# A 0.5 moved into a bias, one row added earlier, fewer sums by DMA, and ScalarE's operand left in the bank where TensorE wrote it

## The chip, the cores and the metric

The kernel runs on one core of a Trainium2 chip. A core has a matrix engine (TensorE, PE in the profile), VectorE (DVE), ScalarE (ACT) and GpSimd (POOL), each with its own queue of instructions that it works off in order, and 16 DMA engines. The metric is the device time of one execution in microseconds, and less is better. A time within 0.5% of the kernel before counts as the same here.

## The reference

The input x holds 64 graphs of 256 nodes with 128 features each, all in float32, and there is one 256 x 256 matrix adj. Four layers follow each other; each takes h = relu(layernorm(x)) and adds its result to x.

```python
# layer 0: five steps of a gated update, h = (1 - z) h + z hv, with adj @ h as message
# layer 1: x + relu([h, A h, A(A h) ...] @ Theta1 + bias)
# layer 2: y = ((adj @ h) + h) @ weight + bias;  x + y / max(norm(y), 1e-12)
# layer 3:
s1 = einsum('bkf,ef->bke', h, W1)          # W = adj, cut in two halves
s2 = einsum('bkf,ef->bke', h, W2)
pre = s1[:, :, None, :] + s2[:, None, :, :] + b_lin
e = einsum('bije,e->bij', leaky_relu(pre, 0.2), a) + adj
x + sigmoid(softmax(e) @ h)
```

Layer 3 is nearly all of the work: for each of 64 graphs it forms 256 x 256 pairs of nodes with 256 channels each, bends them, and sums them over the channels with weights a. The kernel writes sigmoid(v) as 0.5 tanh(v/2) + 0.5, and this last 0.5 is the "0.5 of x" in the title.

## The kernel before, in words

The graphs go through in 32 pairs. For each pair, `front` (L484) computes layers 0 to 2 and prepares layer 3; it is a chain of some 109 steps, each on one engine, with a `yield` between them that names the engine and the time from which the step can run. Front p is begun when pair p - 2 begins to be scored, and the planner spreads its steps over the scores of 1.8 pairs (`SPREAD`), so that two fronts are under way beside the main work. At its end a front leaves the operands of layer 3: s1a, s1b (rows, used as one scalar for each partition), s2c and s2n (copies in SBUF, for GpSimd) and s2a, which stays in the PSUM bank where TensorE projected it, since VectorE reads it from there.

The main work is cut into slots: 64 slots for each pair, 2048 in all, and each has two tiles of 128 x 2048 elements, one for each half of the channels (k = 0 and k = 1). `work_on_tile` (L910) makes a tile: VectorE in one instruction (L930, k = 0 only, from s1a and the bank of s2a), ScalarE in eight instructions (L942, k = 1 only), GpSimd in eight instructions (L947, either half). ScalarE reads its operand in a PSUM bank of its own, `S2P`, that is kept for the whole program: TensorE projects s2n into a common bank, ScalarE copies it to SBUF (L765), and before its first tile of a pair ScalarE copies it again, from SBUF into the bank S2P (L937; L774 for the first pair, whose graphs run alone). There are 14 tile buffers.

`score` (L991) has TensorE sum a tile over its channels, in four groups of 32 columns, into one row of a bank of scores (L1006). One slot in three is "joined" (`SHARE = (1, 3)`, none in the last 96 slots): GpSimd makes its second tile, and issues a DMA that adds this tile onto the first one in SBUF (`add_pair`, L965, the issue is L967); TensorE then scores one tile instead of two. 650 slots are joined.

When the 64 tiles of 32 slots are scored, `tail` (L805) finishes them: two VectorE instructions add the smaller of two rows to the scores in the bank (L812), one adds the row `lin` and writes the sum to SBUF (L816); then come the maximum, the exponential, two transposes by TensorE, a product with h3, tanh on ScalarE (L849), and o = 0.5 tanh + x3 (L853). So x3 must hold the 0.5 already: GpSimd adds it for each pair (L713), behind the layernorm that reads x3.

The order of the whole program is written out by a planner, the loop at the end. It keeps a clock for each engine, gives each step a cost from a table (`ran(engine, us)`), and takes for the engine whose clock is least what is ready: tails first, then fronts, then tiles or scores. Each engine is bound to the resulting order. Costs that matter here: TURN (four transposes) 0.80 us, PROJECT (one tile scored, or one projection) 0.86, norm on GpSimd 1.55, L713 0.7, one issue 0.65, landing of a sum 6.6 after its issue. Eight PSUM banks lie in a list `spare`; `take()` (L121) gives the one that is free the longest, and a step that needs a bank isn't ready while the list is empty.

Of the kernel before, what the change touches and what calls it, by code (L numbers as in the profile page):

```python
# [10 lines left out]
OP = mybir.AluOpType  # L11
# [10 lines left out]
MOST_POSITIVE = -MOST_NEGATIVE  # L22
PE, DVE, ACT, POOL = ENGINES = (mybir.EngineType.PE, mybir.EngineType.DVE, mybir.EngineType.Activation, mybir.EngineType.Pool)
SLOTS = 64
SHARE = (1, 3)
AHEAD_OF = 2
ALONE = 96
LOW = 1
# [4 lines left out]
def kernel(  # L33
# [87 lines left out]
    def take():  # L121

        spare.sort(key=lambda b: b[1])
        return spare.pop(0)
# [139 lines left out]
    def other_constants():  # L264
# [17 lines left out]
        yield DVE, 12.0  # L282
        nc.vector.tensor_add(th[:, 1:3, :], th_raw[:, 1:3, :], th_raw[:, 3:5, :])
        nc.vector.tensor_sub(th[:, 0, :], th_raw[:, 0, :], th[:, 2, :])
        ran(DVE, 0.5)
        yield DVE, clock[DVE]
        small = work.tile([P, 32], F32, name="small", bufs=1)

# [164 lines left out]
    SHORT = dict(tag="short", bufs=12)  # L453


    PROJECT, MIX, TURN, PRODUCT, PRODUCTS = (None, 0.44, 0.86), (None, 0.88, 1.74), (None, 0.55, 0.80), (None, 0.45, 0.88), (None, 1.33, 2.64)
    COPY, BIASED, TANH, ELEMENTS = (None, 0.32, 0.48), (None, 0.40, 0.58), (None, 0.40, 0.57), (None, 0.36, 0.61)
    NORMED, STATS, LAST = (None, 0.78, 1.55), (None, 0.40, 0.8), (None, 0.55, 1.04)

    def norm(src, since, h):  # L460

        nb = src.shape[1]
        stats = work.tile([P, nb * NC, 3], F32, name="stats", bufs=4)
        mv = work.tile([P, nb * NC, 2], F32, name="mv", bufs=4)
        s, h = rows_of(src), rows_of(h)[:, :, 0:D]
        yield DVE, since
        for k in range(0, nb * NC, 2):
            nc.vector.bn_stats(stats[:, k:k + 2, :].rearrange("p k s -> p (k s)"), s[:, k:k + 2, :].rearrange("p k d -> p d k"))
        nc.vector.tensor_reduce(mv[:, :, 0], stats[:, :, 1:2], AX.X, OP.add, negate=True)
        t = ran(DVE, STATS[nb], since) + 0.1  # L470
        yield POOL, t
        inverse_root(mv[:, :, 1], stats[:, :, 2], 1.0 / D, OP.mult, LN_EPS, OP.add)
        nc.gpsimd.tensor_mul(mv[:, :, 0], mv[:, :, 0], mv[:, :, 1])  # L473
        t = ran(POOL, 1.55, t)
        yield ACT, t
        for k in range(nb * NC):
            nc.scalar.activation(h[:, k, :], s[:, k, :], AF.Relu, bias=mv[:, k, 0:1], scale=mv[:, k, 1:2])  # L477
        return ran(ACT, NORMED[nb], t)

    READY = {}  # L480
    S2P = []
    OF_FIRST = {}

    def front(p, batches):  # L484
# [34 lines left out]
        def turned_of(b):  # L519
            return by_token(b[0], nb)  # L520
# [143 lines left out]
        t = ran(DVE, ELEMENTS[nb], t)  # L664
        yield DVE, t
        x2 = token("x2", tag="x12", bufs=3)
        nc.vector.scalar_tensor_tensor(x2, turned_of(po), 0.0, x1, op0=OP.max, op1=OP.add)
        t = ran(DVE, ELEMENTS[nb])
        spare.append([po[0], t])

# [38 lines left out]
        h3 = kept("h3", [NC, D + 1])  # L709
        nc.gpsimd.memset(h3[:, :, :, D:D + 1], 2.0)  # L710
        t = yield from norm(x3, t, h3)
        yield POOL, t
        nc.gpsimd.tensor_scalar(x3, x3, 0.5, None, op0=OP.add)  # L713
        ran(POOL, 0.45 if alone else 0.7, t)
        yield PE, t, 1
        b = take()
        to_feature(b[0], h3)
# [39 lines left out]
        t = moved(t) + 1.5  # L757
        t_lin = t
        yield PE, t_hT, 1
        b = take()  # L760
        project(b[0], w2n[:, P:2 * P], hT)
        t = ran(PE, PROJECT[nb], t_hT, b[1])
        yield ACT, t
        s2n = kept("s2n", [N])
        nc.scalar.copy(s2n, seen(b))  # L765
        t_2 = ran(ACT, COPY[nb], t)
        spare.append([b[0], t_2])
        s2p = []
        if alone:
            yield ACT, t_2, not S2P  # L770
            if not S2P:
                S2P.append(take())
            s2p.append(by_feature(S2P[0][0])[:, own])
            nc.scalar.copy(s2p[0], s2n)  # L774
            ran(ACT, COPY[nb], t_2, S2P[0][1])
        yield PE, t_hT, 1
        b = take()
        project(b[0], w1[:, P:2 * P], hT)
# [12 lines left out]
        nc.scalar.activation(s1a, seen(b), AF.Identity, bias=blin_s[:, 0:1], scale=1.0)  # L791
        t_n = ran(ACT, BIASED[nb], t)
        spare.append([b[0], t_n])
        ops = dict(x3=x3, h3=h3, s1=(s1a, s1b), s2a=seen(s2a), bank=s2a, s2c=s2c, s2n=s2n, s1o=s1o, s2o=s2o, s2p=s2p,
                   lin=lin, t_lin=t_lin, since=(max(t_n, t_s2a), max(t_b, t_2), max(t_b, t_2)), alone=alone,
                   left=SLOTS // 2 if alone else SLOTS)
        for u in batches:
            READY[p, u] = ops
        tiles.extend([t, max(t_b, t_n, t_lin)] for t, _ in lent)

    def across(u):
# [3 lines left out]
    def tail(u, pe, since):  # L805

        ops = READY[u]
        x3, h3, pe, lin = ops["x3"], ops["h3"], [by_feature(pe[0])[:, k, :] for k in range(NB)], ops["lin"]
        yield DVE, max(since, ops["t_lin"])
        sc = feat("sc", **SHORT)  # L810
        for k, (b, c) in enumerate(across(u)):
            nc.vector.scalar_tensor_tensor(pe[k], ops["s2o"][:, b, :], ops["s1o"][:, b, c:c + 1], pe[k], op0=OP.min, op1=OP.add)  # L812
        t = ran(DVE, 0.8, since, ops["t_lin"])
        yield DVE, t
        used = banks_of.pop(u)
        nc.vector.tensor_add(sc, by_feature(used), lin.to_broadcast([P, NB, N]) if ops["alone"] else lin)  # L816
        t = ran(DVE, ELEMENTS[2], t)
        spare.append([used, t])
        yield DVE, t
        nmx = work.tile([P, NB], F32, name="nmx")  # L820
        nc.vector.tensor_reduce(nmx, sc, AX.X, OP.max, negate=True)
        t = ran(DVE, ELEMENTS[2], t)
        yield ACT, t
        for b in range(NB):
            nc.scalar.activation(sc[:, b, :], sc[:, b, :], AF.Exp, bias=nmx[:, b:b + 1], scale=1.0)
        t_s = ran(ACT, 0.8, t)
        yield PE, t_s, 1
        b = take()
        to_token(b[0], sc)
# [12 lines left out]
        t = ran(PE, PRODUCT[2], t, bank[1])  # L842
        yield DVE, t
        rs = work.tile([P, NB], F32, name="rs")
        nc.vector.reciprocal(rs, po[:, :, D])
        t = t_s = ran(DVE, 0.15, t)
        yield ACT, t
        for k in range(NB):
            nc.scalar.activation(po[:, k, 0:D], po[:, k, 0:D], AF.Tanh, scale=rs[:, k:k + 1])  # L849
        t = ran(ACT, 0.5, t, t_s)  # L850
        yield DVE, t
        o = work.tile([P, NB, D], F32, name="o")
        nc.vector.scalar_tensor_tensor(o, po[:, :, 0:D], 0.5, x3[:, 0] if ops["alone"] else x3[:, :, u[1], :], op0=OP.mult, op1=OP.add)  # L853
        t = ran(DVE, 0.36, t)
        spare.append([bank[0], t])
        p, k = u
        nc.sync.dma_start(out[p * NB + k].rearrange("(c p) d -> p c d", p=P) if ops["alone"] else
                          out[p * NB:(p + 1) * NB, k * P:(k + 1) * P, :].rearrange("b p d -> p b d"), o)
        TAILED.add(u)
# [50 lines left out]
    def work_on_tile(e):  # L910
        if e not in begun:
            k = part_of(e)
            tiles.sort(key=lambda t: t[1])
            begun[e] = [slot(k), k, *tiles.pop(0), 0]
            following[k] += 1
            held[e] += 1
            if k == 0:
                READY[where(begun[e][0])[0]]["left"] -= 1
        n, k, t, free, part = begun[e]
        u, r = where(n)  # L920
        ops = READY[u]
# [6 lines left out]
        if e == DVE:  # L928
            whole = [P, 4, NB, N]
            nc.vector.tensor_tensor(t, rows.to_broadcast(whole), ops["s2a"].unsqueeze(1).to_broadcast(whole), op=OP.min)  # L930
            done = ran(DVE, 2.2, since)
            ops["bank"][1] = max(ops["bank"][1], done)
            parts = 1
        elif e == ACT:
            if not ops["s2p"]:
                ops["s2p"].append(by_feature(S2P[0][0]))
                nc.scalar.copy(ops["s2p"][0], ops["s2n"])  # L937
                ran(ACT, 0.62, since)
            parts = 2
            for g in (2 * part, 2 * part + 1):  # L940
                for b in range(NB):
                    nc.scalar.activation(t[:, g, b, :], other(ops["s2p"][0], b), AF.Relu, bias=rows[:, g, b], scale=-1.0)  # L942
            done = ran(ACT, 1.43, since)
        else:
            parts = 4
            for b in range(NB):
                nc.gpsimd.tensor_scalar(t[:, part, b, :], other(ops["s2n" if k else "s2c"], b), rows[:, part, b],  # L947
                                        MOST_NEGATIVE, op0=OP.min, op1=OP.max)
            done = ran(POOL, 0.9, since)
        begun[e][4] += 1  # L950
        if part + 1 == parts:
# [2 lines left out]
                pairs.setdefault(n, {})[k] = done, t, e  # L954
            else:
                made.append((done, n, k, t, e))
        if k == 0 and not ops["left"] and ops["bank"][0] is not None:
            spare.append(list(ops["bank"]))
            ops["bank"][0] = None

    def pair_ready():

# [166 lines left out]
```

## Time and profile before

| | |
|---|---|
| runs | 4886.89, 4869.19, 4869.73 us; median 4869.73 |
| profiled execution | 4870.96 us, its span 4869.2 us |
| granted TensorE clock | 0.997 |
| tiles made | VectorE 1751, ScalarE 1254 (10032 / 8), GpSimd 794 + 297 (6352 / 8, 2376 / 8); 4096 in all |
| tiles scored by TensorE | 3446 (27568 records / 8) |
| sums by DMA | 650, 1024 KB each, median 8.4 us from issue to landing |
| DMA, mean share of 16 engines in the middle of the program | 0.77 to 0.78 |

Each row of the profile's groups gives line, engine and operation, how many instructions, their summed busy time, the mean duration of one, and the idle time of the engine just before them. Durations of neighbours overlap where an engine starts one instruction before the last has ended; what one instruction really takes from its engine is read from the distance of the starts in the timeline.

### The profile page before, as it was taken

What the parts mean: (1) busy time and instruction counts of PE and PEld (TensorE: products, weight loads), DVE (VectorE), ACT (ScalarE), POOL (GpSimd) and SP (SyncE); (2) the same over time, 40 slices, a digit from 0 to 9 for tenths busy, and PEclk for the clock granted to TensorE, in tenths of its full rate; (3) what the DMA queues carried; (4) which work ended last, traced back from release to release, by engine and by line L of the source; (5) the groups of instructions that cost most, each with busy time, mean ns of one, the idle gap of its engine ahead of it and who ended that gap; (6) DMA issues with size and microseconds to landing.
All of it is one profiled execution on the core that took longest, in us unless ns stands there. A gap on an engine that the chain in (4) does not pass through costs nothing.

```text
span 4869.2 us, 134117 instructions
## 1 busy us (share of the span) xinstructions
PE 4729.6 (97%) x52183; PEld 1750.1 (36%) x52183; DVE 4666.6 (96%) x3571; ACT 4630.5 (95%) x12119; POOL 4693.2 (96%) x9914
## 2 busy tenths in 40 slices
PE   9999999999999999999999999999999999999999
PEld 4333333333333333333333333333333333333333
DVE  6999999999999999999999999999999999999998
ACT  6999999999999999999999999999999999999999
POOL 3999999999999999999999999999999999999998
PEclk9999999999999999999999999999999999999999
DMA  1778777777777787777877777877777777787830
GB/s 46 158 148 165 159 155 160 158 153 163 156 158 156 149 165 160 153 162 152 165 160 155 160 153 156 166 156 155 163 147 162 161 160 157 154 163 155 165 65 5
DMA packets 138729, 725.21 MB, mean 149 GB/s; under 512 B 15721, under 2 KB 50921, under 8 KB 54889
## 3 DMA queue, kind: packets, MB, share of 16 engines
q0 software_dynamic: 93600, 681.62, 69.9%
q1 hardware_dynamic: 43768, 35.01, 2.5%
q8 instruction: 408, 6.68, 0.5%
q14 instruction: 233, 1.90, 0.1%
q10 hardware_dynamic: 720, 0.00, 0.0%
HBM read 26.48 MB, written 8.52 MB: 7 GB/s over the span
## 4 chain that ended last, share of the span: by engine, by line
PE 48%; POOL 16%; DVE 15%; DMA 10%; ACT 6%; issue 4%; POOLq 0%; DVEq 0%; SPq 0%; ACTq 0%
PE bank L1006 29%; PE bank L402 17%; POOL rl L947 13%; DVE rl L930 12%; DMA rl<-rl 10%; ACT rl L942 4%; POOL rl L967 1%; PE bank L433 1%; PE bank L425 1%; POOL mv L397 1%; DVE hT L616 1%; DVE bank L612 0%; ACT h L477 0%; DVE d L608 0%; DVE rh L573 0%
## 5 line engine op out<-in xcount | busy, mean ns | idle before, releaser
L930 DVE TENSOR_TENSOR rl<-s1a,bank 128x2048 f32<-128x2048 f32 x1751 | 3921.6, 2279 | 105.7 <-DMA rl<-rl 75.4
L942 ACT ACTIVATE rl<-bank,s1b 128x256 f32<-128x256 f32 x10032 | 3946.2, 691 | 75.4 <-DMA rl<-rl 48.1
L947 POOL TENSOR_SCALAR rl<-s2n,s1b 128x256 f32<-128x256 f32 x6352 | 3043.6, 789 | 28.4 <-DMA rl<-rl 8.6
L1006 PE MATMUL bank<-rl,win_n 128*32 128x512 f32 x17536 | 2209.3, 594 | 49.0 <-DMA rl<-rl 46.3
L1006 PE MATMUL bank<-rl,win 128*32 128x512 f32 x10032 | 1331.7, 594 | 0.0
L947 POOL TENSOR_SCALAR rl<-s2c,s1a 128x256 f32<-128x256 f32 x2376 | 1155.4, 747 | 5.0 <-DMA rl<-rl 0.7
L1006 PEld LDWEIGHTS bank<-rl,win_n 128*32 128x32 f32 x17536 | 568.9, 110 | 1195.5 <-issue 929.9
L967 POOL DMA_DIRECT2D rl<-rl x650 | 689.4, 1077 | 9.4 <-PE bank L1006 2.2
L1006 PEld LDWEIGHTS bank<-rl,win 128*32 128x32 f32 x10032 | 330.3, 110 | 637.1 <-issue 525.3
L402 PE MATMUL bank<-mT,wts 128*32 128x512 f32 x2480 | 324.9, 592 | 0.2 <-ACT mT L525 0.2
L402 PE MATMUL bank<-adj_t,h 128*32 128x256 f32 x4960 | 299.0, 380 | 7.8 <-ACT h L627 7.6
L402 PEld LDWEIGHTS bank<-adj_t,h 128*32 128x32 f32 x4960 | 160.3, 110 | 170.0 <-issue 42.8
L477 ACT ACTIVATE h<-x,mv 128x128 f32<-128x128 f32 x376 | 162.7, 572 | 41.3 <-POOL mv L473 41.2
L402 PE MATMUL bank<-rh,u5t 128*32 128x512 f32 x1240 | 162.1, 593 | 8.0 <-DVE rh L573 7.9
L402 PE MATMUL bank<-hT,wts 128*32 128x512 f32 x1240 | 164.1, 596 | 0.0
L402 PE MATMUL bank<-mT,w 128*32 128x512 f32 x1240 | 162.4, 593 | 0.4 <-ACT bank L569 0.4
L569 ACT ACTIVATE bank<-bank,gate_b 128x512 f32<-128x512 f32 (+1 forms) x165 | 138.5, 840 | 20.9 <-PE bank L402 13.6
L402 PEld LDWEIGHTS bank<-mT,wts 128*32 128x32 f32 x2480 | 81.6, 110 | 186.0 <-issue 149.6
L397 POOL TENSOR_TENSOR mv<-mv,minus_half 128x4 f32<-128x4 f32 (+1 forms) x132 | 134.0, 1015 | 11.0
L525 ACT COPY mT<-bank 128x512 f32<-128x512 f32 x155 | 119.5, 771 | 26.2 <-PE bank L402 26.0
L592 ACT ACTIVATE bank<-bank,gate_b 128x512 f32<-128x512 f32 (+1 forms) x165 | 134.1, 813 | 10.2 <-PE bank L402 9.9
L433 PE MATMUL bank<-ident,hT 128*128 128x128 f32 x620 | 101.5, 286 | 38.1 <-DVE hT L616 37.8
(206 smaller groups left out, 3354.9 us busy)
## 6 DMA issues: line engine op xcount, KB each, us to landing
rl<-rl POOLq DMA_DIRECT2D x650, 1024.0 KB, 8.4
rows<-row SPq DMA_DIRECT2D x31, 512.0 KB
xin<-in_x_dram SPq DMA_DIRECT2D x64, 128.0 KB
out_dram<-o SPq DMA_DIRECT2D x64, 128.0 KB
row<-quarter SPq DMA_DIRECT2D x62, 2.0 KB
rows<-row SPq DMA_DIRECT2D x2, 256.0 KB
w_raw<-in_L_gnn_w_w_dram SPq DMA_DIRECT2D x3, 128.0 KB
rl<-in_L_gnn_Theta_dram SPq DMA_DIRECT2D x1, 320.0 KB
```

What stands on the lines that cost most here:

```text
L397: nc.gpsimd.tensor_tensor(t, t, minus_half[:, 0:t.shape[1]], op=OP.pow)
L402: nc.tensor.matmul(o[g:g + 32], w[:, g:g + 32], t, start=start, stop=stop, skip_group_check=True)
L433: nc.tensor.transpose(pt[:, b, c, :], ht[:, b, c * P:(c + 1) * P], ident)
L477: nc.scalar.activation(h[:, k, :], s[:, k, :], AF.Relu, bias=mv[:, k, 0:1], scale=mv[:, k, 1:2])
L525: nc.scalar.copy(c, seen(bank))
L569: nc.scalar.activation(seen(r), seen(pr), AF.Tanh, bias=br, scale=0.5)
L592: nc.scalar.activation(seen(pr), seen(pr), AF.Tanh, bias=bz, scale=0.5)
L930: nc.vector.tensor_tensor(t, rows.to_broadcast(whole), ops["s2a"].unsqueeze(1).to_broadcast(whole), op=OP.min)
L942: nc.scalar.activation(t[:, g, b, :], other(ops["s2p"][0], b), AF.Relu, bias=rows[:, g, b], scale=-1.0)
L947: nc.gpsimd.tensor_scalar(t[:, part, b, :], other(ops["s2n" if k else "s2c"], b), rows[:, part, b], MOST_NEGATIVE, op0=OP.min, op1=OP.max)
L967: nc.gpsimd.dma_start(out=t.rearrange("p g b n -> p (g b n)"), in_=z.rearrange("p g b n -> p (g b n)"), accum_op=OP.add)
L1006: nc.tensor.matmul(pe[g * 32:(g + 1) * 32, :], w[:, 31 - r:63 - r], flat(t[:, g]), start=False, stop=(left[u] == 0), skip_group_check=True)
```

## The change

Six places change; the tiles, the weights and the sums stay what they are.

1. The bias of layer 1 gets 0.5 added once, and the relu of layer 1 becomes max(v + 0.5, 0.5), so that x carries the 0.5 from layer 1 on. The layernorms behind it don't see a constant. GpSimd's L713 is gone.
2. The second projection of s2 stays in its bank, `s2b`, and ScalarE reads its tiles' operand there. The bank S2P and the copies into it (L937, L774) are gone. Each pair (each graph, in the first pair) now holds two banks, s2a and s2b, from its projection until the last tile that reads it is begun.
3. SHARE goes from (1, 3) to (4, 13): 600 of the first 1952 slots are joined instead of 650.
4. In the tail the row `lin` is added first, in place in the bank, by one instruction; the two instructions with the smaller of two rows come second and write to SBUF.
5. Costs of the planner: TURN 0.80 to 0.60, statistics 0.8 to 0.87, norm on GpSimd 1.55 to 1.69, tanh of the tail 0.5 to 0.9 (some of them for a single graph as well).
6. A bank of either kind is given back when no tile that reads it is left or under way.

```diff
-SHARE = (1, 3)
+SHARE = (4, 13)
...
+        nc.vector.tensor_scalar(bias1, bias1, 0.5, None, op0=OP.add)
...
-    PROJECT, MIX, TURN, ... = (None, 0.44, 0.86), (None, 0.88, 1.74), (None, 0.55, 0.80), ...
+    PROJECT, MIX, TURN, ... = (None, 0.44, 0.86), (None, 0.88, 1.74), (None, 0.38, 0.60), ...
-    NORMED, STATS, LAST = (None, 0.78, 1.55), (None, 0.40, 0.8), (None, 0.55, 1.04)
+    NORMED, STATS, LAST = (None, 0.78, 1.55), (None, 0.50, 0.87), (None, 0.55, 1.04)
...
-        t = ran(POOL, 1.55, t)
+        t = ran(POOL, 1.69, t)
...
-        nc.vector.scalar_tensor_tensor(x2, turned_of(po), 0.0, x1, op0=OP.max, op1=OP.add)
+        nc.vector.scalar_tensor_tensor(x2, turned_of(po), 0.5, x1, op0=OP.max, op1=OP.add)
...
-        yield POOL, t
-        nc.gpsimd.tensor_scalar(x3, x3, 0.5, None, op0=OP.add)
-        ran(POOL, 0.45 if alone else 0.7, t)
...
-        b = take()
-        project(b[0], w2n[:, P:2 * P], hT)
+        s2b = take()
+        project(s2b[0], w2n[:, P:2 * P], hT)
...
-        spare.append([b[0], t_2])
-        s2p = []
-        if alone:
-            yield ACT, t_2, not S2P
-            if not S2P:
-                S2P.append(take())
-            s2p.append(by_feature(S2P[0][0])[:, own])
-            nc.scalar.copy(s2p[0], s2n)
-            ran(ACT, COPY[nb], t_2, S2P[0][1])
...
+        used = banks_of.pop(u)
+        nc.vector.tensor_add(by_feature(used), by_feature(used), lin.to_broadcast([P, NB, N]) if ops["alone"] else lin)
...
         for k, (b, c) in enumerate(across(u)):
-            nc.vector.scalar_tensor_tensor(pe[k], ops["s2o"][:, b, :], ops["s1o"][:, b, c:c + 1], pe[k], op0=OP.min, op1=OP.add)
-        nc.vector.tensor_add(sc, by_feature(used), lin.to_broadcast([P, NB, N]) if ops["alone"] else lin)
+            nc.vector.scalar_tensor_tensor(sc[:, k, :], ops["s2o"][:, b, :], ops["s1o"][:, b, c:c + 1], pe[k], op0=OP.min, op1=OP.add)
...
-        t = ran(ACT, 0.5, t, t_s)
+        t = ran(ACT, 0.9, t, t_s)
...
-            if not ops["s2p"]:
-                ops["s2p"].append(by_feature(S2P[0][0]))
-                nc.scalar.copy(ops["s2p"][0], ops["s2n"])
-                ran(ACT, 0.62, since)
...
-                    nc.scalar.activation(t[:, g, b, :], other(ops["s2p"][0], b), AF.Relu, bias=rows[:, g, b], scale=-1.0)
+                    nc.scalar.activation(t[:, g, b, :], other(ops["s2b"], b), AF.Relu, bias=rows[:, g, b], scale=-1.0)
             done = ran(ACT, 1.43, since)
+            ops["bank"][1][1] = max(ops["bank"][1][1], done)
...
-        if k == 0 and not ops["left"] and ops["bank"][0] is not None:
-            spare.append(list(ops["bank"]))
-            ops["bank"][0] = None
+        if k < 2 and not ops["left"][k] and ops["bank"][k] and not any(b[1] == k and where(b[0])[0] == u for b in begun.values()):
+            spare.append(ops["bank"][k])
+            ops["bank"][k] = None
```

More of the change, by code (lines that the diff above doesn't have):

```diff
@@ L284, in other_constants @@
         nc.vector.tensor_sub(th[:, 0, :], th_raw[:, 0, :], th[:, 2, :])
-        ran(DVE, 0.5)
+        nc.vector.tensor_scalar(bias1, bias1, 0.5, None, op0=OP.add)
+        ran(DVE, 0.7)
         yield DVE, clock[DVE]
@@ L453 @@
     SHORT = dict(tag="short", bufs=12)
-    PROJECT, MIX, TURN, PRODUCT, PRODUCTS = (None, 0.44, 0.86), (None, 0.88, 1.74), (None, 0.55, 0.80), (None, 0.45, 0.88), (None, 1.33, 2.64)
+    PROJECT, MIX, TURN, PRODUCT, PRODUCTS = (None, 0.44, 0.86), (None, 0.88, 1.74), (None, 0.38, 0.60), (None, 0.45, 0.88), (None, 1.33, 2.64)
     COPY, BIASED, TANH, ELEMENTS = (None, 0.32, 0.48), (None, 0.40, 0.58), (None, 0.40, 0.57), (None, 0.36, 0.61)
-    NORMED, STATS, LAST = (None, 0.78, 1.55), (None, 0.40, 0.8), (None, 0.55, 1.04)
+    NORMED, STATS, LAST = (None, 0.78, 1.55), (None, 0.50, 0.87), (None, 0.55, 1.04)
     def norm(src, since, h):
@@ L480 @@
     READY = {}
-    S2P = []
     OF_FIRST = {}
@@ L759, in front @@
         yield PE, t_hT, 1
-        b = take()
-        project(b[0], w2n[:, P:2 * P], hT)
-        t = ran(PE, PROJECT[nb], t_hT, b[1])
+        s2b = take()
+        project(s2b[0], w2n[:, P:2 * P], hT)
+        t = ran(PE, PROJECT[nb], t_hT, s2b[1])
         yield ACT, t
         s2n = kept("s2n", [N])
-        nc.scalar.copy(s2n, seen(b))
+        nc.scalar.copy(s2n, seen(s2b))
         t_2 = ran(ACT, COPY[nb], t)
-        spare.append([b[0], t_2])
-        s2p = []
-        if alone:
-            yield ACT, t_2, not S2P
-            if not S2P:
-                S2P.append(take())
-            s2p.append(by_feature(S2P[0][0])[:, own])
-            nc.scalar.copy(s2p[0], s2n)
-            ran(ACT, COPY[nb], t_2, S2P[0][1])
         yield PE, t_hT, 1
@@ L793, in front @@
         spare.append([b[0], t_n])
-        ops = dict(x3=x3, h3=h3, s1=(s1a, s1b), s2a=seen(s2a), bank=s2a, s2c=s2c, s2n=s2n, s1o=s1o, s2o=s2o, s2p=s2p,
+        ops = dict(x3=x3, h3=h3, s1=(s1a, s1b), s2a=seen(s2a), s2b=seen(s2b), bank=[s2a, s2b], s2c=s2c, s2n=s2n, s1o=s1o, s2o=s2o,
                    lin=lin, t_lin=t_lin, since=(max(t_n, t_s2a), max(t_b, t_2), max(t_b, t_2)), alone=alone,
-                   left=SLOTS // 2 if alone else SLOTS)
+                   left=[0, 0])
         for u in batches:
             READY[p, u] = ops
+            for n in range(p * SLOTS + u * SLOTS // 2, p * SLOTS + (u + 1) * SLOTS // 2):
+                ops["left"][0] += 1
+                ops["left"][1] += n not in WITH
         tiles.extend([t, max(t_b, t_n, t_lin)] for t, _ in lent)
@@ L809, in tail @@
         yield DVE, max(since, ops["t_lin"])
+        used = banks_of.pop(u)
+        nc.vector.tensor_add(by_feature(used), by_feature(used), lin.to_broadcast([P, NB, N]) if ops["alone"] else lin)
+        t = ran(DVE, ELEMENTS[2], since, ops["t_lin"])
+        yield DVE, t
         sc = feat("sc", **SHORT)
         for k, (b, c) in enumerate(across(u)):
-            nc.vector.scalar_tensor_tensor(pe[k], ops["s2o"][:, b, :], ops["s1o"][:, b, c:c + 1], pe[k], op0=OP.min, op1=OP.add)
-        t = ran(DVE, 0.8, since, ops["t_lin"])
-        yield DVE, t
-        used = banks_of.pop(u)
-        nc.vector.tensor_add(sc, by_feature(used), lin.to_broadcast([P, NB, N]) if ops["alone"] else lin)
-        t = ran(DVE, ELEMENTS[2], t)
+            nc.vector.scalar_tensor_tensor(sc[:, k, :], ops["s2o"][:, b, :], ops["s1o"][:, b, c:c + 1], pe[k], op0=OP.min, op1=OP.add)
+        t = ran(DVE, 0.8, t)
         spare.append([used, t])
@@ L916, in work_on_tile @@
             held[e] += 1
-            if k == 0:
-                READY[where(begun[e][0])[0]]["left"] -= 1
+            if k < 2:
+                READY[where(begun[e][0])[0]]["left"][k] -= 1
         n, k, t, free, part = begun[e]
@@ L931, in work_on_tile @@
             done = ran(DVE, 2.2, since)
-            ops["bank"][1] = max(ops["bank"][1], done)
+            ops["bank"][0][1] = max(ops["bank"][0][1], done)
             parts = 1
         elif e == ACT:
-            if not ops["s2p"]:
-                ops["s2p"].append(by_feature(S2P[0][0]))
-                nc.scalar.copy(ops["s2p"][0], ops["s2n"])
-                ran(ACT, 0.62, since)
             parts = 2
```

## The prediction

> **What bounds the kernel now.** I read the busy times and the chain of the page first, then the timeline for what an operation really takes, then the waits.
>
> ```profile
> PE 4729.6 (97%) x52183; PEld 1750.1 (36%) x52183; DVE 4666.6 (96%) x3571; ACT 4630.5 (95%) x12119; POOL 4693.2 (96%) x9914
> PE 48%; POOL 16%; DVE 15%; DMA 10%; ACT 6%; issue 4%; POOLq 0%; DVEq 0%; SPq 0%; ACTq 0%
> L1006 PE MATMUL bank<-rl,win_n 128*32 128x512 f32 x17536 | 2209.3, 594 | 49.0 <-DMA rl<-rl 46.3
> L1006 PE MATMUL bank<-rl,win 128*32 128x512 f32 x10032 | 1331.7, 594 | 0.0
> L967 POOL DMA_DIRECT2D rl<-rl x650 | 689.4, 1077 | 9.4 <-PE bank L1006 2.2
> ```
>
> No engine stands out: four of them are 95 to 97% busy, and the chain passes from one to the next, half of it on PE. Whatever is taken from one engine alone can be lost on the others, so I need each engine's true load. The chain in order of time gives PE's:
>
> ```profile
> 2052.71 4.29 PE bank L1006 x40
> ...
> 2068.03 0.59 PE bank L433 x4
> ...
> 2099.30 4.35 PE bank L402 x128
> ```
>
> 40 records are five tiles: 0.858 us a tile, with PE working without a gap; four transposes (L433) take 0.59. Counted with these: 27568 records of tiles / 8 x 0.858 = 2957 us; 7192 records of 128x512 projections at the same rate, 771; 8960 of 128x256 at half of it (0.43 for eight; 32 of them are 1.73 in the same view), 482; 1252 transposes / 4 x 0.59 = 185; 6264 small ones of 128x128 and 128x129 at 0.22 for eight (L734 in the same view), 172; the rest some 35. PE's true load is 4602 us, 94.5% of the span.
>
> The Trainium skill (Perfetto Trace Analysis, its opening note) says that matmul busy time is a bad measure of closeness to the limit because matmuls are pipelined. The rows agree, with 594 ns for one and 0.858 us for eight. By the busy time PE would have 140 us left, by the starts 267.
>
> The timeline gives the others:
>
> ```profile
> 2143.09 2.72 POOL L947 TENSOR_SCALAR rl<-s2c,s1a 128x256 f32<-128x256 f32 x6
> 2145.89 1.51 POOL L713 TENSOR_SCALAR x<-x 128x512 f32<-128x512 f32 x1
> 2147.48 0.92 POOL L947 TENSOR_SCALAR rl<-s2c,s1a 128x256 f32<-128x256 f32 x2
> 2148.34 0.87 POOL L967 DMA_DIRECT2D rl<-rl  x1
> 2148.97 3.81 POOL L947 TENSOR_SCALAR rl<-s2n,s1b 128x256 f32<-128x256 f32 x8
> ```
> ```profile
> 2043.76 0.59 ACT L937 COPY bank<-s2n 128x512 f32<-128x512 f32 x1
> 2044.38 1.57 ACT L942 ACTIVATE rl<-bank,s1b 128x256 f32<-128x256 f32 x4
> ```
>
> From start to start L713 costs POOL 1.59 us, an issue (L967) 0.63 (its 1077 ns run on beside the next tile), and L937 costs ACT 0.62. POOL's idle time is 176 us of the span, 78 of it in the first 120 us, and it waits for almost nobody afterwards; the others wait for it and for the sums that it issues:
>
> ```profile
> PEld bank L1006 <- DMA rl<-rl: 102.4, 90, 3.7
> DVE rl L930 <- DMA rl<-rl: 75.4, 60, 3.8
> PEld bank L1006 <- POOL rl L947: 62.8, 168, 2.1
> ACT h L477 <- POOL mv L473: 48.5, 45, 2.9
> ACT rl L942 <- DMA rl<-rl: 48.1, 28, 4.4
> PE bank L1006 <- DMA rl<-rl: 46.3, 41, 2.8
> ```
>
> So the three engines that make tiles set the pace together, POOL and its sums foremost, with PE some 5% behind them in load but first on the chain whenever its queue is full.
>
> **The change part by part.** All against this execution, 4870.96 us, 1.23 above the median.
>
> *L713 gone.* 31 x 1.59 + 2 x 0.95 (the half-size form lasts 862 ns) = -51 us of POOL. What replaces it is one instruction before the main work, and another constant in L667: 0.
>
> *Fewer sums.* POOL issues 50 less: -50 x 0.63 = -31. PE scores 50 tiles more: +50 x 0.858 = +43. The number of tiles made stays 4096.
>
> *Copies into S2P gone.* 31 x 0.62 + 2 x 0.6 = -20 us of ACT. The tile instructions read a bank before and after: 0.
>
> *Tail.* The same three DVE instructions in another order, each with one operand in the bank as before, and one now writes the bank where it wrote SBUF. L812 (128x256) takes 487 ns writing the bank, L816 (128x512) 682 ns writing SBUF, and L612 (128x512), which writes the bank, 692: 64 x 10 ns is below 1 us, either way. 0.
>
> *Sum for the makers.* POOL -82, ACT -20; the planner gives tiles to whichever maker is free, so the 102 us spread over three: **-34 us**. If they stayed on POOL alone and another engine set the pace, it would be nearer to -82 x 16% (POOL's share of the chain) = -13; that is the other end.
>
> *The tiles more on PE.* Between 0 (they fall into its 267 us of slack) and +43 (each lies on the path). I take PE's share of the chain, 48%: **+21**.
>
> *Sums fewer.* The four waits for landed sums above, with POOL's own 9, add up to 281 us over four engines; 50/650 of that is 22, a quarter of it 5 for the span. The chain has 10%, 487 us, on landings; 50/650 of that is 37. With the DMA engines' share down from 0.77 to about 0.72 a landing should also be a little quicker than 8.4 us. Nearer to the small end, since a chain that loses a landing goes on over another engine: **-12**.
>
> *The planner's costs.* TURN is 0.80 in the table and 0.59 in the trace; ten of them in a pair, 32 pairs: the order of before is laid out for 64 us of PE time that aren't used. L713 is 0.7 in the table and 1.59 in the trace, so POOL runs late by 0.9 us in each pair, and the layernorm's 1.55 is 1.70 (2058.87 to 2060.57 in POOL's timeline), four times in a pair. After, both fit. Late POOL work costs the rows <-POOL above (63 + 49, a quarter for the span: 28); at best all of it goes, -28. But PE's 64 us were also a cushion, in which PE caught up with late tiles; at PE's 48% its loss could cost +31. Where the two ends are so alike I take a little more for the lateness, since it is waits that the trace shows: **-8**.
>
> *Banks.* Before, S2P is one bank for good, and s2a is held from about 12 of 109 steps before a front's end until the pair's last k = 0 tile is begun. A front lasts 1.8 pairs and ends 0.2 of a pair early (about 30 us of the 150 that a pair takes, 4869 / 32 = 152 with the start), so two s2a overlap for some 45 us. After, two s2b overlap as well, for about 30 us of each 150: then four of eight banks are held, one or two are scores, and two or three remain for the other front and the tails, where three or four remained. No row of before names a wait for a bank, since the planner puts it in the order. Below it is bounded by 0; no gain, because S2P is one bank and s2b never less than one. Above by one step of a front (1.8 x 150 us / 109 = 2.5 us) in which PE stands still at each pair: 31 x 2.5 = +77. PE always has tiles to score in that time, so near 0: **+4**.
>
> The Trainium skill (PSUM — Partial Sum Buffer, its summary of rules) speaks against this part: "Evacuate promptly — 2 MiB is tight". The page gives no price; by it one would expect the +77 rather than the +4. No run here has shown which it is.
>
> *Sum.* -34 + 21 - 12 - 8 + 4 = **-29 us**, or 4842 for the profiled execution and **4841** beside the median.
>
> **The rivals.**
>
> 1. *Balanced (same).* PE's tiles weigh in full (+43) and the makers give the -34 and the landings -12: 4867. For it: PE has the largest share of the chain, and the four true loads are alike. Against it: PE's 267 us of slack, and its waits for sums and POOL (102 + 46 + 63), which get fewer.
>
> 2. *PE becomes the bound (slower).* PE rises to 4602 + 43 = 4645, and the planner, which now plans 64 us less for transposes, leaves PE no cushion: +43 + 31 for PE's part, the makers' gain is only the -13 of POOL's share, -12 for landings, and +4 for banks: +53, that is 4923 at its worst; about 4907 if half of the cushion is kept. It decides from the point at which PE is over about 96% loaded by starts in the middle of the program. Against it: the last 170 us, where nothing is joined and PE is 100% busy from 4700 to 4800 in the view by stretches, are such a stretch already, and DVE, ACT and POOL are 96 to 99% busy beside it there.
>
> 3. *Banks run short.* Two or three free banks don't carry a front and a tail; fronts fall behind, tiles of the next pair come late, and the wait shows as tile makers waiting for s1a and s1b. Up to the +77 less the -29, without the +4 that it replaces: 4914. It decides if the waits come in the last 30 us before each new pair.
>
> 4. *It does less than it says.* The makers' gain is not shared out: -13 + 21 - 12 + 4 = 0: 4870. This counts as the same.
>
> **How the numbers follow.** The forecast (over 0.5% faster, below 4845, which is about what a measurement of this kernel can tell from no change) has 0.44; rivals 1 and 4 together 0.34 (0.20 and 0.14); rival 2 0.15, rival 3 0.07, and these two make slower 0.22. The low end takes the makers' -34 with PE's tiles free, the landings at -25 and the lateness at -20: -79, or 4791. The high end, 4905, reaches nearly to rival 2 with half of the cushion, and leaves out the worst of 2 and 3, some 0.13. The forecast's own range is 4791 to 4845.
>
> **What would show it.** L713 and L937 gone; L967 x600; PE records 27968 on L1006. POOL's tiles up by some 15 to 25 over 1091, with DVE's and ACT's down. PE's waits for landed sums below 100 + 46 us and the waits for POOL below 63 and 49 show the forecast right; PE's share of the chain over 60% and its busy share over 98% show rival 2; a new wait of L942 or L947 for s1b in each pair, or of PE on front steps by readers of a bank, shows rival 3. If the waits for POOL stay and POOL's load doesn't fall, the sharing was wrong, which is rival 4.

## The result and the profile after

The changed kernel takes 4805.16 us (median of 4, 4804.58 to 4806.42), the kernel before 4869.47 beside it: a ratio of 0.986, 95% interval 0.9838 to 0.9881 (the two medians give 0.9868). That is faster, as forecast and inside the range, but by 64 us where the sum gave 29. The kernel before takes about 4870 us in some series of runs and about 4887 in others, and not every kernel was seen to shift with it, so a difference of under 0.4% between ratios from different series is not settled here.

The page of the changed kernel, the lines that answer those of before (L994 is now the scoring, L955 the issue of a sum, L929, L921 and L935 are the tiles of ScalarE, VectorE and GpSimd):

```profile
span 4802.8 us, 134800 instructions
PE 4742.3 (99%) x52583; PEld 1743.3 (36%) x52583; DVE 4650.0 (97%) x3567; ACT 4590.1 (96%) x12030; POOL 4640.6 (97%) x9927
PE 69%; DVE 9%; POOL 9%; DMA 6%; ACT 4%; issue 2%; POOLq 0%; DVEq 0%; ACTq 0%
L994 PE MATMUL bank<-rl,win_n 128*32 128x512 f32 x17992 | 2214.4, 594 | 27.7 <-DMA rl<-rl 16.3
L955 POOL DMA_DIRECT2D rl<-rl x600 | 644.5, 1090 | 3.1 <-POOL rl L935 1.5
rl<-rl POOLq DMA_DIRECT2D x600, 1024.0 KB, 8.3
```

TensorE has 50 tiles more and is still through 66 us earlier: its load by starts is 4602 + 43 = 4645 us, 96.7% of the span where it was 94.5%. L713 and L937 are gone. A sum lands almost as late as before (8.3 us after its issue, 8.4 before). What has changed is who waits for it. These are the six rows that the prediction shows of before, in the order of their size now:

```profile
PEld bank L994 <- POOL rl L935: 55.7, 178, 1.6
PEld bank L994 <- DMA rl<-rl: 53.7, 60, 3.0
ACT h L478 <- POOL mv L474: 35.5, 40, 2.5
DVE rl L921 <- DMA rl<-rl: 27.7, 30, 2.8
ACT rl L929 <- DMA rl<-rl: 26.9, 24, 2.6
PE bank L994 <- DMA rl<-rl: 16.3, 20, 2.1
```

With GpSimd's own 7.3 the waits for landed sums are 132 us, where they were 281; the prediction had taken off 22. TensorE's two rows, of weight loads (PEld) and of matmuls (PE), name mostly the same stretches: by the starts and ends in the trace, 42 of the 46.3 us of before lie inside the 102.4, so all totals here count such stretches twice. The waits for GpSimd's tiles and layernorms have shrunk only from 62.8 and 48.5 to 55.7 and 35.5, and the weight loads' wait for VectorE's tiles has grown from 36.8 to 77.3.

Two more rows have fallen, which the prediction doesn't show although the first is longer than any that it does. In them TensorE waits, before a transposition in a front, for VectorE's hT. Before:

```profile
PEld bank L433 <- DVE hT L616: 127.5, 108, 3.5
PE bank L433 <- DVE hT L616: 37.8, 39, 2.6
```

After:

```profile
PEld bank L434 <- DVE hT L616: 71.3, 74, 2.9
PE bank L434 <- DVE hT L616: 8.9, 14, 2.0
```

So the missing gain is to be looked for in two places, TensorE's waits in the fronts and the waits for sums. The experiments ask which part of the change took them away.

### The profile page after: what moved, and what is told of

Its sections match the earlier page's. It is cut to its first block, busy times and chain, and to the rows that moved or that the text cites. A ratio compares the mean times of both kernels' runs of the same rounds, so it can differ in the third digit from the quotient of the medians.

```text
span 4802.8 us, 134800 instructions
## 1 busy us (share of the span) xinstructions
PE 4742.3 (99%) x52583; PEld 1743.3 (36%) x52583; DVE 4650.0 (97%) x3567; ACT 4590.1 (96%) x12030; POOL 4640.6 (97%) x9927
## 4 chain that ended last, share of the span: by engine, by line
PE 69%; DVE 9%; POOL 9%; DMA 6%; ACT 4%; issue 2%; POOLq 0%; DVEq 0%; ACTq 0%
PE bank L994 42%; PE bank L403 23%; POOL rl L935 8%; DVE rl L921 8%; DMA rl<-rl 6%; ACT rl L929 3%; PE bank L434 2%; PE bank L426 1%; POOL rl L955 1%; ACT h L478 0%; POOL mv L398 0%; DVE d L608 0%; DVE rh L573 0%; DVE bank L612 0%; DVE hT L616 0%
## 5 line engine op out<-in xcount | busy, mean ns | idle before, releaser
L929 ACT ACTIVATE rl<-bank,s1b 128x256 f32<-128x256 f32 x9976 | 3963.3, 774 | 56.9 <-DMA rl<-rl 26.9
L921 DVE TENSOR_TENSOR rl<-s1a,bank 128x2048 f32<-128x2048 f32 x1746 | 3907.9, 2276 | 52.1 <-DMA rl<-rl 27.7
L935 POOL TENSOR_SCALAR rl<-s2n,s1b 128x256 f32<-128x256 f32 x6408 | 3065.8, 807 | 21.5 <-DMA rl<-rl 7.3
L994 PE MATMUL bank<-rl,win_n 128*32 128x512 f32 x17992 | 2214.4, 594 | 27.7 <-DMA rl<-rl 16.3
L994 PE MATMUL bank<-rl,win 128*32 128x512 f32 x9976 | 1298.5, 594 | 0.0
L935 POOL TENSOR_SCALAR rl<-s2c,s1a 128x256 f32<-128x256 f32 x2416 | 1171.9, 756 | 4.2 <-PE bank L994 0.3
L994 PEld LDWEIGHTS bank<-rl,win_n 128*32 128x32 f32 x17992 | 566.5, 110 | 1224.2 <-issue 978.7
L955 POOL DMA_DIRECT2D rl<-rl x600 | 644.5, 1090 | 3.1 <-POOL rl L935 1.5
L994 PEld LDWEIGHTS bank<-rl,win 128*32 128x32 f32 x9976 | 316.6, 110 | 626.6 <-issue 500.7
L569 ACT ACTIVATE bank<-bank,gate_b 128x512 f32<-128x512 f32 (+1 forms) x165 | 147.8, 896 | 24.0 <-PE bank L403 19.1
L525 ACT COPY mT<-bank 128x512 f32<-128x512 f32 x155 | 136.4, 880 | 20.6 <-PE bank L403 20.4
L592 ACT ACTIVATE bank<-bank,gate_b 128x512 f32<-128x512 f32 (+1 forms) x165 | 139.7, 847 | 13.8 <-PE bank L403 13.6
L605 ACT ACTIVATE bank<-bank,gate_b 128x512 f32<-128x512 f32 x155 | 133.6, 862 | 6.9 <-PE bank L403 6.7
```

Of the source, the lines that this page charges most:

```text
L525: nc.scalar.copy(c, seen(bank))
L569: nc.scalar.activation(seen(r), seen(pr), AF.Tanh, bias=br, scale=0.5)
L592: nc.scalar.activation(seen(pr), seen(pr), AF.Tanh, bias=bz, scale=0.5)
L605: nc.scalar.activation(seen(pv), seen(pv), AF.Tanh, bias=bh_n, scale=-1.0)
L929: nc.scalar.activation(t[:, g, b, :], other(ops["s2b"], b), AF.Relu, bias=rows[:, g, b], scale=-1.0)
L955: nc.gpsimd.dma_start(out=t.rearrange("p g b n -> p (g b n)"), in_=z.rearrange("p g b n -> p (g b n)"), accum_op=OP.add)
```

## The experiments

Three theories stood against each other. **Load**: the work taken from GpSimd and ScalarE brings the gain (the prediction's sum). **Sums**: fewer sums land earlier. **Order**: the planner's costs are most of it. After the first four runs a fourth was formed, the **pair**: share and costs each need the other. Each run is told as a ratio to the kernel before in its own series. In the tables, TensorE's waits for sums are its two rows (weights and matmuls) added, the makers' those of ScalarE, VectorE and GpSimd.

### One part alone

The share alone:

```diff
-SHARE = (1, 3)
+SHARE = (4, 13)
```

> The kernel before with SHARE (4, 13) alone. Load theory (the work taken from GpSimd and ScalarE brings the gain): +21 for the tiles more on TensorE, -12 for landings, -10 for GpSimd's 31 us shared by three, so about 4869, the same. Sums theory (fewer sums in flight land earlier, and that is most of the gain): 4820 to 4835, with the waits for landed sums near half of the 281 us. Order theory (the planner's costs are most of it): TensorE is the longest engine in a plan with 0.80 for TURN, so 43 us more on it show in full: about 4900.

Measured 1.0038 (1.0026 to 1.0051), slower. The planner's four costs alone:

```diff
-TURN ... (None, 0.55, 0.80); STATS ... (None, 0.40, 0.8); norm 1.55; tanh 0.5
+TURN ... (None, 0.38, 0.60); STATS ... (None, 0.50, 0.87); norm 1.69; tanh 0.9
```

> The kernel before with the planner's new costs alone (TURN, statistics, norm, tanh); each instruction does what it did. Order theory: most of the 64 us, 4810 to 4830. Load theory: -8, about 4862. Sums theory: no change in the landings, so 4862 to 4870, or slower, since TensorE has less of a cushion when sums land late: up to 4900.

Measured 1.0043 (1.003 to 1.0055), slower too. The 0.5 in the bias of layer 1, without L713, alone:

```diff
-        yield POOL, t
-        nc.gpsimd.tensor_scalar(x3, x3, 0.5, None, op0=OP.add)
-        ran(POOL, 0.45 if alone else 0.7, t)
```

> The kernel before without L713, the 0.5 in the bias of layer 1 alone. Load theory: -51 us of GpSimd, a third of it shared or 16% of it, -8 to -17: 4853 to 4861. Sums theory: GpSimd issues sums earlier, up to 0.9 us in each pair late in plan: 4840 to 4860. Order theory: below 0.3%, 4856 to 4870.

Measured 0.9969 (0.9957 to 0.998): 15 us, within the range by load and within that by sums too; TensorE's waits for sums fall from 149 to 90 us beside it. And ScalarE's operand left in its bank, with S2P and its copies gone, alone:

```diff
-            nc.scalar.activation(t[:, g, b, :], other(ops["s2p"][0], b), AF.Relu, bias=rows[:, g, b], scale=-1.0)
+            nc.scalar.activation(t[:, g, b, :], other(ops["s2b"], b), AF.Relu, bias=rows[:, g, b], scale=-1.0)
```

> The kernel before with s2b read in its bank by ScalarE, and without S2P and the copies into it, alone. Load theory: -20 us of ScalarE, -7 shared, +4 for banks: 4866 to 4870. Bank shortage (the third rival of the prediction): slower, up to 4914, with waits just before each new pair. A gain of over 15 us would be more than ScalarE's copies can give by load.

Measured 1.0015 (1.0006 to 1.0024): a little slower, far from the 4914 of a shortage.

| alone | ratio | TensorE's waits for sums, us | makers' waits for sums, us |
|---|---|---|---|
| before | 1 | 149 | 133 |
| share | 1.0038 | 22 | 187 |
| costs | 1.0043 | 262 | 93 |
| without L713 | 0.9969 | 90 | 126 |
| bank | 1.0015 | 143 | 138 |

The four ratios add up to a loss of 0.65%, the whole change is a gain of 1.4%. Neither the sums theory (4820 to 4835 for the share) nor the order theory (4810 to 4830 for the costs) stands, though each came near the loss of the other's part (about 4900 for the share by order, up to 4900 for the costs by sums). The two losing parts show in opposite places. With the share alone, the rows of the waits read:

```profile
ACT rl L942 <- DMA rl<-rl: 105.2, 45, 7.0
DVE rl L930 <- DMA rl<-rl: 71.1, 59, 3.7
PEld bank L1006 <- DMA rl<-rl: 17.0, 25, 3.5
```

With the costs alone:

```profile
PEld bank L1006 <- DMA rl<-rl: 178.4, 145, 4.4
PE bank L1006 <- DMA rl<-rl: 84.1, 85, 3.5
DVE rl L930 <- DMA rl<-rl: 52.1, 40, 5.1
ACT rl L942 <- DMA rl<-rl: 32.6, 22, 4.3
```

One cause can stand behind both; it is argued here from the rows. In the plan a sum is seen 0.65 + 0.13 + 6.6 = 7.4 us after its issue begins; on the chip the median is 8.4, and the earliest 6.7. So somebody comes a microsecond too early at the median. If the plan has TensorE busy with transposes that take less (0.80 for 0.59) and with more tiles, TensorE is late in the plan, and the makers, ScalarE above all, are the ones that are sent to a buffer just as the sum out of it is planned to land. If the plan knows the transposes and has few tiles for TensorE, TensorE is the one that is sent to the sum at that moment.

### Share and costs together, and each taken back

Both diffs above, of the share and of the costs, on the kernel before:

> The kernel before with SHARE (4, 13) and the planner's new costs, nothing else. Alone they cost 19 and 22 us. If parts simply add: 4870 + 41 = 4911. Pair theory (the costs let TensorE come to sums before they land, and fewer sums are only paid back if the plan gives TensorE the time; each needs the other): 4815 to 4850, with TensorE's waits for landed sums well below the 262 us that they have with the costs alone, and ScalarE's below the 105 us that they have with the share alone. Load theory: nothing is taken from GpSimd here but 50 issues, so 4855 to 4870.

Measured 0.9967 (0.9954 to 0.9979): a gain of 0.33% where the parts add up to a loss of 0.81%. Put on the 4870 of the expectation this is 4854, between the ranges of the pair theory (up to 4850) and of the load theory (from 4855), and the interval reaches into both. What it settles is that the two parts don't add: the measured 4871.93 us stand against the 4911 of the sum even undivided by the 4887.23 of the kernel before beside them. Then the changed kernel with one part taken back at a time:

```diff
-SHARE = (4, 13)
+SHARE = (1, 3)
```

> The changed kernel with SHARE back at (1, 3), all the rest as changed. Pair theory: TensorE is ahead of its sums again, 4860 to 4890, its waits for landed sums above 150 us. Load theory: GpSimd has 31 us more of issues, TensorE 43 less, about 4800 to 4815.

Measured 0.9931 (0.9916 to 0.9945), between the two ranges, with 196 us of TensorE's waits for sums.

The four costs taken back (the diff of the costs above, reversed):

> The changed kernel with the planner's old costs (TURN 0.80, statistics 0.8, norm 1.55, tanh 0.5). Pair theory: the plan has TensorE as its longest engine, so the tile makers wait for buffers, as with the share alone: 4850 to 4890. Load theory: +8, about 4813.

Measured 0.999 (0.9981 to 0.9999): without the new costs nearly the whole gain is gone, as the pair theory had it.

The bank S2P back:

```diff
+            s2p.append(by_feature(S2P[0][0])[:, own])
+            nc.scalar.copy(s2p[0], s2n)
...
+                nc.scalar.copy(ops["s2p"][0], ops["s2n"])
```

> The changed kernel with the bank S2P and the copies into it back (s2b given back at once), all the rest as changed. If the parts add: the bank alone cost 7 us, so 4798. If ScalarE's 20 us count once TensorE is no longer held up: 4810 to 4825.

Measured 0.9856 (0.9842 to 0.9871), by the ratio no different from the changed kernel's 0.986. In us it is 4817.24 beside a kernel before of 4887.23, and no changed kernel ran beside it, so a cost or gain of the bank below 0.4% stays open.

The old tail, which adds `lin` last and writes SBUF with it:

```diff
-        nc.vector.tensor_add(by_feature(used), by_feature(used), lin...)
+        nc.vector.tensor_add(sc, by_feature(used), lin...)
```

> The changed kernel with the old order of the tail's three instructions. Prediction's term: nothing, 0.986 within 0.15%. If the tail is the part that makes the 0.5 and the row worth more than their load: 0.990 or above.

Measured 0.9856 (0.984 to 0.9872): no worth of the tail's order shows.

Of the costs, one was taken back alone:

```diff
-TURN ... (None, 0.38, 0.60)
+TURN ... (None, 0.55, 0.80)
```

> The changed kernel with TURN alone planned at the old 0.55 and 0.80. If TURN is what the old costs did (0.999 with all four back): 0.996 to 1.000, TensorE's waits for landed sums near 10 us and ScalarE waiting for them for 70. If the other three costs (norm 1.55, statistics 0.8, tanh 0.5) are most of it: 0.987 to 0.990.

Measured 0.9969 (0.9956 to 0.9981), with 20 us of TensorE's waits for sums and 149 of the makers': TURN is most of what the old costs do (0.999 with all four).

| changed kernel with | ratio | TensorE's waits | makers' waits |
|---|---|---|---|
| all as changed | 0.986 | 70 | 62 |
| SHARE (1, 3) | 0.9931 | 196 | 85 |
| all old costs | 0.999 | 8 | 156 |
| old TURN | 0.9969 | 20 | 149 |
| S2P | 0.9856 | 89 | 70 |
| old tail | 0.9856 | 58 | 55 |

What TURN does is seen best where TensorE's matmuls stand still. The rows of their waits (PE alone), added by what the matmul is for:

| kernel | before matmuls of fronts and tails, us | before matmuls of tiles, us |
|---|---|---|
| before | 85 | 48 |
| share alone | 117 | 8 |
| costs alone | 41 | 102 |
| share and costs | 42 | 52 |
| all as changed | 28 | 27 |
| changed, old TURN | 88 | 6 |
| changed, all old costs | 103 | 3 |

With the old costs TensorE waits in the fronts, with the new ones and the old share it waits at the tiles, most of it for sums; only the new share with the new costs keeps both low. In the run with the old TURN the waits for hT are back:

```profile
PEld bank L434 <- DVE hT L616: 115.8, 103, 3.9
PE bank L434 <- DVE hT L616: 33.6, 42, 3.0
```

Why transpositions that are planned too long leave TensorE waiting for hT was not tested. Nor was what a new order is worth by itself: each of these runs has another order of the whole program, and the two whose work hardly changes, the bank alone and the old tail, moved by 0.15% and by nothing that shows.

### GpSimd's 0.5: its load, or its lateness

L713 was planned at 0.7 us and took 1.59. If the load matters, putting it back costs the same however it is planned.

The three lines of L713 back in the changed kernel:

> The changed kernel with GpSimd's 0.5 (the old L713) back, planned at 0.7 us as before; times as a ratio to the kernel before, where the changed kernel is 0.986. Load theory: 51 us of GpSimd over three makers, +17 us or 0.35%: 0.9895. Lateness theory (GpSimd runs 0.9 us late in each pair, issues sums late, and TensorE waits for them): more than its load, 0.993 to 0.998, with TensorE's waits for landed sums above 100 us where the changed kernel has 70.

Measured 0.9928 (0.9913 to 0.9943), 139 us of TensorE's waits for sums. Then the same with its true cost:

```diff
-        ran(POOL, 0.45 if alone else 0.7, t)
+        ran(POOL, 0.95 if alone else 1.6, t)
```

> As the one above, but planned at 1.6 us, what it takes in the trace (0.95 for a single graph). Lateness theory: only the load is left, 0.988 to 0.990, and TensorE's waits for landed sums near 70 us. Load theory: the same as the one above, within 0.2%.

Measured 0.9897 (0.9882 to 0.9911), 120 us. Half of the loss goes by a true cost with every instruction kept: 51 us of GpSimd are worth about 0.37% by load (0.31% in us, 4820.01 against 4805.16), as the load theory has it, and 0.31% more because the plan didn't know of them. TensorE's waits fell less than the lateness theory said (120, not 70); the makers' fell from 67 to 46.

The whole change without any work taken away but 50 issues (the diffs of the share, of the costs and of L713's cost, on the kernel before):

> The kernel before with SHARE (4, 13), the new costs, and L713 planned at the 1.6 us that it takes: no instruction's work is taken away but 50 issues, L713 and the copies into S2P stay. If the plan is what brings the gain: 0.988 to 0.991, as with GpSimd's 0.5 back and truly planned (0.9897), since the bank and the tail are worth nothing by themselves. If the work taken away is most of it: 0.994 to 0.997, near the share and the costs alone (0.9967).

Measured 0.9924 (0.9907 to 0.9942; the two medians, 4856.00 and 4888.02, give 0.9934), between the two ranges: about half of the gain comes from the plan and the 50 issues fewer, with L713's true cost a part of it.

### The landing itself

If sums that land later than planned are the common cause, the planner can be told of it.

```diff
-ISSUE, ADDED, LANDED, SLACK = 0.65, 5.3, 6.6, 0.3
+ISSUE, ADDED, LANDED, SLACK = 0.65, 5.3, 7.8, 0.3
```

On the kernel before with the new costs:

> The kernel before with the new costs and a landing planned 7.8 us behind its issue in place of 6.6; the costs alone gave 1.0043. If the loss there is TensorE's waits for sums that land later than planned: 0.990 to 0.998, the waits down from 262 us to below 130. If the loss is the load (sums too many for GpSimd and the DMA engines): 1.000 to 1.006.

Measured 0.9997 (0.9988 to 1.0007), TensorE's waits for sums 158 us: the loss of the costs alone (1.0043) goes, and the time ends just below the range for loads, above the one for waits. A landing planned later takes this loss away, but 158 of the 262 us stay, where the theory had below 130. Whether it would gain as much with the old costs, or with the share alone, was not tried, so the late landing as the common cause of both losses is not shown.

On the changed kernel, the same diff, and then 9.0 in place of 7.8:

> The changed kernel with the planner's landing of a sum at 7.8 us behind its issue in place of 6.6. Lateness theory: TensorE's remaining 70 us of waits for landed sums fall below 40, 0.980 to 0.985. If these waits cost nothing: 0.986 or slower, since buffers are held longer in the plan, up to 0.992.

Measured 0.9845 (0.983 to 0.986), 27 us of TensorE's waits, both as the lateness theory had them.

> The changed kernel with the landing planned at 9.0 us. With 7.8 it is 0.9845. If planned landing past the real one costs nothing: 0.983 to 0.985, TensorE's waits for sums near 10 us. If the buffers held longer in the plan weigh: 0.986 to 0.992, with more waits of the tile makers.

Measured 0.9832 (0.9817 to 0.9846), 4792.66 us, the fastest of all and probably faster than the changed kernel by 0.3%. Its waits for landed sums, all four rows:

```profile
DVE rl L921 <- DMA rl<-rl: 10.5, 13, 2.0
ACT rl L929 <- DMA rl<-rl: 9.3, 8, 3.7
PEld bank L994 <- DMA rl<-rl: 4.2, 9, 0.9
POOL rl L935 <- DMA rl<-rl: 0.2, 1, 0.2
```

24 us are left of 281, though a sum lands at 8.3 us as in the changed kernel. Its chain by engine:

```profile
PE 85%; POOL 5%; DVE 4%; ACT 3%; issue 1%; DMA 1%; POOLq 0%; DVEq 0%; ACTq 0%
```

TensorE now carries nearly the whole chain, with a load of 4645 of 4791 us, 97.0%. Is TensorE's load the bound, then? Two runs change it, one to each side:

```diff
-SHARE = (4, 13)
+SHARE = (2, 7)
```

> The changed kernel with the landing planned at 7.8 us and SHARE (2, 7), some 557 sums, 43 us more of tiles on TensorE less 0: its load by starts 97.7% of 4795. If TensorE is the bound now: 0.988 to 0.994. If the sums still are: 0.979 to 0.984.

Measured 0.9849 (0.9834 to 0.9864). With 557 sums (43 fewer) TensorE has 37 us more, and the time is within the intervals of the one with (4, 13) and the same 7.8 us (0.9845): in neither range, so TensorE's load as the bound is not shown.

```diff
-SHARE = (4, 13)
+SHARE = (1, 3)
```

> The changed kernel with the landing planned at 9.0 us and SHARE back at (1, 3). With (4, 13) the chain has 85% on TensorE and TensorE is 97% loaded by starts. If TensorE's load alone is the bound now: 43 us less, 0.974 to 0.980. If the makers and the sums stand just behind it: 0.983 to 0.990, with ScalarE's, VectorE's or TensorE's waits for sums back above 100 us together.

Measured 0.9911 (0.9895 to 0.9928): 43 us less on TensorE, and slower, a little above the second range. The makers stand just behind TensorE, but not by waits for sums, which are 66 us together, where that range had over 100; it is VectorE's and GpSimd's tiles that TensorE waits for:

```profile
PEld bank L994 <- DVE rl L921: 125.7, 196, 3.3
PEld bank L994 <- POOL rl L935: 108.9, 249, 2.3
PE bank L994 <- DVE rl L921: 28.8, 39, 2.4
ACT h L478 <- POOL mv L474: 42.5, 47, 2.8
PEld bank L994 <- DMA rl<-rl: 39.3, 46, 2.9
```

With (4, 13) and the same 9.0 the first three rows are 59.1, 75.4 and 5.4 us. A joined slot binds GpSimd for its second tile and the issue, so that GpSimd may be the late one at one in three, and VectorE late in turn; this is argued only, since no run lightens GpSimd alone at (1, 3).

## Why the prediction was right or wrong

**Right: that no engine stood out, and the true loads.** TensorE at 94.5% by starts could take the 43 us: it is at 96.7% now, and the span shrank. (That TensorE stood "some 5% behind" the makers in load doesn't follow from the prediction's own figures, 94.5% beside 95 to 96% busy.) **Right: L713.** Its removal gave 15 us alone, where the load's share of the makers' term was 17. **Right: the tail**, 0.9856 with the old order against 0.986. **Nearly right: the bank**, priced at -7 and +4, so -3; alone it measured +7, in the changed kernel nothing that shows (0.9856 with S2P back). The Trainium skill says of PSUM "Evacuate promptly — 2 MiB is tight" (PSUM — Partial Sum Buffer, its summary of rules). In these runs the +77 that the prediction had put beside this rule didn't come: with the bank alone, two banks held for each pair in place of the copies cost 0.15%.

**Right in sign: the makers.** GpSimd lost 53 us of busy time, ScalarE 40 and VectorE 17, so the relief was shared, and GpSimd's tiles rose by 12 (1091 to 1103) where 15 to 25 were expected. No run prices the -34 by itself.

**Wrong: the planner's costs, -8, between -28 and +31.** This is the step that failed. It measured +21 us alone (0.43%) and -63 in the changed kernel (0.999 against 0.986). The prediction took the 64 us of TURN for a cushion whose loss cost something, and bounded the gain by the rows that wait for GpSimd, 28 us at most. The rows that these costs moved are others: TensorE's waits for hT, 165 us before (127.5 and 37.8), 80 after, and 149 with TURN put back alone; and the waits for sums, which the new costs raise on TensorE and lower on the makers. It named the right quantity, a plan that believes TensorE slower than it is, and asked neither where TensorE waits under such a plan nor whom it sends too early to a late sum.

**Wrong: the share as a term by itself, +21 for tiles, -12 for landings and a third of -31 for issues, so about -1.** Alone it measured +19 us (0.38%), in the changed kernel -35 (0.9931 against 0.986). Share and costs together are 1.14% better than their sum by the ratios, 0.8% by the us as measured. The whole sum was built of terms that add; these two don't. The -12 priced the waits for sums by the number of sums. They depend on the plan as well: 24 us with 600 of them planned at 9.0 us, 132 with the same 600 planned at 6.6. Its 281 us also added TensorE's two rows, which mostly name the same stretches.

**The rivals.** The sign by which rival 2 was to be known, a chain with over 60% on TensorE and TensorE busy over 98%, came true with the kernel faster: 69% and 98.7%, and 85% of the chain in the fastest run. So this sign didn't tell a kernel that TensorE slows from one in which little else holds TensorE up. Rival 3 didn't come: no new row of waits for a bank appeared in the changed kernel, and it is 0.9856 with S2P back. With the bank alone (0.15% slower) its sign shows faintly: TensorE's weight loads at L402 wait 12.7 us for ScalarE's s1b, which reads a bank, where it was 1.4; whether this is the cost was not tested.

**What stays open.** Why the old TURN with (4, 13) costs a full 1.1% isn't settled row by row: TensorE's matmuls wait 60 us more in the fronts (88 for 28) and 21 less at the tiles, the makers' waits for sums rise from 62 to 149 us, and ScalarE, busy 4590 us in the changed kernel, is busy 4563 there, with 11918 instructions for 12030, so the tiles go to others; these were not separated.

## What to carry to other kernels

Where a fixed order is laid out from a table of costs, compare each cost with the starts in the trace, too high ones as much as too low ones, and the landings of DMAs too. Read the longest waits of every engine before pricing such a change, also where they seem to have nothing to do with it. Change a cost and the division of work that was chosen under it together, since each alone can lose what both gain. And read a chain that moves onto one engine together with the total: here it went with a falling time, as that engine was held up less.

## What the runs showed of the hardware

An accumulating DMA of 1024 KB within SBUF landed 8.4 us after its issue at the median in the kernel before and 8.3 in the changed one (from 6.6 to over 14), with the mean share of the DMA engines at 0.77 and 0.73. Over all runs the medians go from 7.9 us with 557 of them to 8.7 with 650; in the pairs of runs that differ by the share alone, fewer sums landed 0.1 to 0.5 us sooner (8.4 and 8.0 with the share alone, 8.6 and 8.1 with the costs). So the easing that the prediction had hoped for is there, and small: the share alone was slower with it. A GpSimd instruction over 128x512 that adds a constant took 1.59 us from start to start, more than three of its 128x256 tile instructions at 0.45.
